# Loading the projection once and reordering the constants of a Fourier attention and mixture-of-experts kernel

## Chip, cores and metric

The kernel runs on one core of a Trainium2 chip. The core has five engines with instruction queues of their own: PE (TensorE, matrix products; PEld is its weight load), DVE (VectorE), ACT (ScalarE), POOL (GpSimd) and SP (SyncE, which here only issues DMA copies). The metric is device time in microseconds of one execution. A measurement is the median of several runs.

## What is computed

One transformer layer on x of shape (8, 512, 128): linear attention with random Fourier features over 16 heads of 8 dimensions, layer norm, then a top-2-of-8 mixture of experts (128 to 512 to 128), layer norm.

```python
q = (x @ Wq.T + bq).reshape(B, L, 16, 8)      # k and v likewise
p = einsum('blhd,dm->blhm', q, proj) / sqrt(8)
q_prime = concat([cos(p), sin(p)], -1) / sqrt(128)   # k_prime likewise
kv  = einsum('blhm,blhd->bhmd', k_prime, v)
out = einsum('blhm,bhmd->blhd', q_prime, kv)
x = layernorm(x + out.reshape(B, L, 128) @ Wo.T + bo)
route = top2(softmax(x @ Wr + br)), made to sum to 1
x = layernorm(x + sum_e route_e * (relu(x @ W1_e + b1_e) @ W2_e + b2_e))
```

The same projection, 8 x 128, serves all 16 heads.

## The kernel before

**Layout.** All work is in float32. A sequence (512 rows) is held as four chunks of 128 rows. The products that make the phases work on 32 partitions, which are four heads of 8; so the kernel keeps a block-diagonal projection `pbd`, 128 partitions by NJ * M = 4 * 128 columns: row 8h + d holds row d of proj in the column block j = h mod 4 and zeros elsewhere. `npbd` is its negative. `mask` (128 x 4) says which column block a partition belongs to; it comes from the identity `ident` by a sum on DVE (L144).

**Start.** Ahead of the planned work stands a preamble (L116 to L306):

- `load_x(0)` on SP's queue; the four weights Wq, Wk, Wv, Wo, one copy each, on ACT's queue into the tile `first` (L119).
- proj is copied 16 times, once for each head, by 16 copies on SP's queue (L150); DVE multiplies it with `mask` to `pbd` (L153) and negates it to `npbd` (L162).
- POOL fills the constants (columns such as `magic`, `halfpi`, `one`; `once`, `up`, `down`; `vm` and `kv`; `zero`, `below`, `page0` and others) and issues the copies of bv, bo, br, Wr and b2. These instructions are written on `nc.gpsimd`, whose order the framework may change.
- b1, bq and bk are copied as rows into `brow` (L184) on ACT's queue.
- `load_x(1)`, then for each expert a copy of W1 into a combined DRAM array `wcat` and one of W2 into the tile `w2` (L210), then `load_x(2)`, all on SP's queue.
- PE transposes the four weights, DVE copies them to `wT`; PE transposes `brow`, DVE copies it to `bcol` and scales two columns to `bqk`.
- POOL clears `bdiag` (L297), DVE writes b1 onto its diagonals (L298) and the negative of b1 to `nb1c` (L302), which SP stores into `wcat`.

**Planned part.** Everything after that is a list of tasks with an engine, an estimated duration, a due time counted in steps and predecessors. `Plan.make` (L1267) puts them into one order, by simulating the engines with those estimates; the wrapper `InOrder` (L70) then keeps each engine to this order. [...] The PSUM tiles of one bank each, four of them at first (L96, `banks`), are handed to tasks by the planner.

For each sequence there is a preparation (x transposed to `xT`; k, v and q by products with `wT`; `kT` written by DVE, `qT` and `xT` by ACT; `xb` = x + bo on POOL) and NS = 8 steps, four for the keys and four for the queries. A step is a phase product (`p_phase`, into the PSUM tiles `p`, called PE "p" in the profile), the turning into range and the sine and cosine (DVE and ACT), and the products with `vm` or `kv` (PE "bank"). In the first 24 steps (`TURNED`, three sequences) PE does the range reduction itself, by adding a large number, taking it off again and multiplying with `npbd`. Behind the steps come output projection, norm, routing, a scatter of rows to expert pages in DRAM, and the experts' products; pages are worked through in three groups of 4, 3 and 1 sequences.

**The shift.** Relu is done as a maximum with -b1, so what is missing is added back as one row for each expert, b1_e @ W2_e + b2_e. `prepare_shift` plans it: eight groups of four products of `bdiag` with `w2` (`p_shift`), DVE's sum with b2 (`v_shift`), the rows spread over partitions (`p_rows`, `v_rows`) and stored to `wcat`. The first group has no predecessor (`last = None`) and is due at step 9.6; in the trace one group runs ahead of k's product of sequence 0.

Of the kernel before, what the change touches and what calls it, by code (L numbers as in the profile page):

```python
# [18 lines left out]
ROUND = 12582912.0  # L19
# [6 lines left out]
def kernel(  # L26
# [57 lines left out]
    pe, act, dve, pool = (InOrder(e) for e in (nc.tensor, nc.scalar, nc.vector, nc.gpsimd))  # L84
# [14 lines left out]
    def mm(*args, **kwargs):  # L99
        pe.matmul(*args, **kwargs)  # L100

    def tr(*args):
        pe.transpose(*args)
# [12 lines left out]
    load_x(0)  # L116
    first = feat.tile([P, NG * 512], F32, tag="r", name="first")
    wnat = first[:, 0 : 4 * D].rearrange("p (i d) -> p i d", d=D)
    for i, w in enumerate((Wq, Wk, Wv, Wo)):  # L119
        nc.scalar.dma_start(out=wnat[:, i, :], in_=w)  # L120

    ident = const.tile([P, P], F32, name="ident")
    make_identity(nc, ident)

    def column(value, name):
        t = const.tile([P, 1], F32, name=name)
        nc.gpsimd.memset(t, value)
        return t
# [6 lines left out]
    mone = column(-1.0, "mone")  # L135
    one = column(1.0, "one")
    euler = column(math.e, "euler")
    low = column(-3e38, "low")

    def small_wide(t):  # L140
        return t.to_broadcast([P, NC])


    mask = const.tile([P, NJ], F32, name="mask")  # L144
    nc.vector.tensor_reduce(
        mask, ident.rearrange("p (g j d) -> p j g d", j=NJ, d=DH), AX.XY, ALU.add
    )

    prep = first[:, 4 * D : 4 * D + M]
    for h in range(H):  # L150
        nc.sync.dma_start(out=prep[DH * h : DH * (h + 1), :], in_=proj)
    pbd = const.tile([P, NJ * M], F32, name="pbd")
    nc.vector.tensor_tensor(  # L153
        pbd.rearrange("p (j m) -> p j m", m=M),
        prep.unsqueeze(1).to_broadcast([P, NJ, M]),
        mask.unsqueeze(2).to_broadcast([P, NJ, M]),
        ALU.mult,
    )


    npbd = const.tile([P, NJ * M], F32, name="npbd")
    nc.vector.tensor_scalar(npbd, pbd, -1.0, None, ALU.mult)  # L162
    once = const.tile([P, P], BF16, name="once")
    nc.gpsimd.memset(once, 1.0)
    up = const.tile([P, 1], BF16, name="up")
    nc.gpsimd.memset(up, ROUND / 32)
    down = const.tile([P, 1], BF16, name="down")
    nc.gpsimd.memset(down, -ROUND / 32)


    XW = D + DH
    vm = const.tile([P, NC, NJ * XW], F32, name="vm")
    nc.gpsimd.memset(vm, 0.0)
    kv = const.tile([P, 2, NJ * XW], F32, name="kv")
    nc.gpsimd.memset(kv, 0.0)

    def blocks(t):
        return t.rearrange("p c (j x) -> p c j x", x=XW)[:, :, :, 0:D].rearrange(
            "p c j (g y) -> p c j g y", y=32
        )[:, :, :, :, 0:DH]  # L180

    NB = E * NF
    brow = first[0 : NB + 2, 4 * D + M : 4 * D + M + P]
    nc.scalar.dma_start(out=brow[0:NB, :], in_=b1.rearrange("e (c f) -> (e c) f", f=P))  # L184
    nc.scalar.dma_start(out=brow[NB : NB + 1, :], in_=bq.unsqueeze(0))
    nc.scalar.dma_start(out=brow[NB + 1 : NB + 2, :], in_=bk.unsqueeze(0))

    bvb = const.tile([P, D], F32, name="bvb")
    nc.gpsimd.dma_start(out=bvb, in_=bv.partition_broadcast(P))
    bob = const.tile([P, D], F32, name="bob")  # L190
    nc.gpsimd.dma_start(out=bob, in_=bo.partition_broadcast(P))
    brb = const.tile([P, E], F32, name="brb")
    nc.gpsimd.dma_start(out=brb, in_=br.partition_broadcast(P))
    wr = const.tile([P, E], F32, name="wr")
    nc.gpsimd.dma_start(out=wr, in_=Wr)
    b2s = const.tile([E, D], F32, name="b2s")
    nc.gpsimd.dma_start(out=b2s, in_=b2)


    desc = const.tile([P, NC, E], F32, name="desc")  # L200
    for e in range(E):
        nc.gpsimd.memset(desc[:, :, e : e + 1], float(E - e))

    load_x(1)

# [2 lines left out]
    wcat = tc.dram_tile([E, P, WN + NF + D], F32, name="wcat")  # L208
    w2 = const.tile([P, E, NF * D], F32, name="w2")
    for e in range(E):  # L210
        nc.sync.dma_start(out=wcat[e, :, 0:FF], in_=W1[e])
        nc.sync.dma_start(
            out=w2[:, e, :].rearrange("p (c d) -> p c d", d=D),
            in_=W2[e].rearrange("(c p) d -> p c d", p=P),
        )
# [11 lines left out]
    assert L % P == 0  # L227
    DY = D + 1
    zero = const.tile([P, 8, DY], F32, name="zero")
    nc.gpsimd.memset(zero, 0.0)  # L230
    nc.gpsimd.memset(zero[:, :, D:DY].bitcast(I32), 1 << 30)
    ys_d = [tc.dram_tile([n * P, DY], F32, name=f"ys_{i}") for i, n in enumerate(pages)]
    rows = [2 * L * n for n in GROUPS]
    res_d = [tc.dram_tile([n, D], F32, name=f"res_{i}") for i, n in enumerate(rows)]
# [4 lines left out]
    row_of = const.tile([P, max(GROUPS), 2, NC], I32, name="row_of")  # L239
    for m in range(max(GROUPS)):  # L240
        for k in range(2):
            nc.gpsimd.iota(
                row_of[:, m, k, :],
                pattern=[[2, NC]],
                base=2 * L * m + k,
                channel_multiplier=2 * NC,
            )

    def clear(i, e):
# [8 lines left out]


    ones = const.tile([P, P], BF16, name="ones")  # L260
    nc.gpsimd.memset(ones, 1.0)
    ltri = const.tile([P, P], BF16, name="ltri")
    nc.gpsimd.affine_select(
        ltri, ones, pattern=[[1, P]], compare_op=ALU.is_gt, fill=0.0, base=0, channel_multiplier=-1
    )

    below = const.tile([P, E + 1, E], F32, name="below")
    nc.gpsimd.memset(below, 0.0)
    for e in range(E):
        nc.gpsimd.memset(below[:, e + 1, 0 : e + 1], 1.0)  # L270

    page0 = const.tile([P, len(GROUPS), E], F32, name="page0")
    for i in range(len(GROUPS)):
        for e in range(E):
            nc.gpsimd.memset(page0[:, i, e : e + 1], float(full[i] * e))
    ramp_i = const.tile([P, max(NT)], I32, name="ramp_i")
    nc.gpsimd.iota(ramp_i, pattern=[[1, max(NT)]], base=0, channel_multiplier=0)
    ramp = const.tile([P, max(NT)], F32, name="ramp")
    nc.gpsimd.tensor_copy(ramp, ramp_i)


    PH = [ps_p.tile([P, 2, 512], F32, tag=f"p{n}", name=f"p_{n}") for n in range(2)]
    P4 = [PH[g // 2][:, g % 2, :] for g in range(NG)]
    for i in range(4):
        tr(P4[0][:, ts(i)], wnat[:, i, :], ident)
    wT = const.tile([P, 4, D], F32, name="wT")
    dve.tensor_copy(wT.rearrange("p i d -> p (i d)"), P4[0])
    tr(P4[2][:, 0 : NB + 2], brow, ident[: NB + 2, : NB + 2])
    bcol = const.tile([P, NB + 2], F32, name="bcol")
    dve.tensor_copy(bcol, P4[2][:, 0 : NB + 2])  # L290
    scale = 1.0 / (2.0 * math.pi * math.sqrt(DH))
    bqk = const.tile([P, 2], F32, name="bqk")
    dve.tensor_scalar(bqk, bcol[:, NB : NB + 2], scale, None, ALU.mult)


    bdiag = const.tile([P, NF, E * E], F32, name="bdiag")
    nc.gpsimd.memset(bdiag, 0.0)  # L297
    nc.vector.tensor_copy(  # L298
        bdiag[:, :, :: E + 1], bcol[:, 0:NB].rearrange("p (e c) -> p c e", c=NF)
    )  # L300
    nb1c = const.tile([P, NB], F32, name="nb1c")
    nc.vector.tensor_scalar(nb1c, bcol[:, 0:NB], -1.0, None, ALU.mult)  # L302
    nc.sync.dma_start(
        out=wcat[:, :, WN : WN + NF].rearrange("e p c -> p e c"),
        in_=nb1c.rearrange("p (e c) -> p e c", c=NF),
    )  # L306
# [86 lines left out]
        )  # L393

    def prepare_shift():
        last = None
        for e in range(E):
            last = plan.add(
                "PE", 1.05, lambda bank, e=e: p_shift(bank, e), due=9.6 + e / 4,
                after=[last], bank="shift",  # L400
            )
        last = plan.add("DVE", 0.3, v_shift, due=12, after=[last], bank="shift", free="shift")
        done = []
        for e in (0, 4):
            t = plan.add("PE", 1.1, lambda bank, e=e: p_rows(bank, e), due=12.5, after=[last], bank=("rows", e))
            done.append(plan.add(
                "DVE", 0.7, lambda bank, e=e: v_rows(bank, e), due=13, after=[t],
                bank=("rows", e), free=("rows", e), ring=("r", "rows", 2),
            ))
            last = t  # L410
        t = plan.add("SP", 0.4, store_rows, due=13, after=done, land=5)
        plan.give("r", "rows", [t], lag=5)
        return t
# [788 lines left out]

    all_groups = [Group(i) for i in range(len(GROUPS))]
    seqs = [Sequence(b) for b in range(B)]
    shift_done = prepare_shift()
    clears = [(i, e) for i in range(len(GROUPS)) for e in range(E)]
    for b, s in enumerate(seqs):
        s.prepare()
        s.steps()
        for k in range(NS):  # L1210
            if clears and NS * b + k >= 1:
                i, e = clears.pop(0)
                all_groups[i].clears.append(
                    plan.add(
                        "SP", 0.3, lambda i=i, e=e: clear(i, e), due=NS * b + k,
                        after=[s.t_p[k]], land=8,
                    )
                )
# [141 lines left out]
def ts(i, size=128):  # L1360
    return slice(i * size, (i + 1) * size)
# [32 lines left out]
```

## Time and profile before

| | us |
|---|---|
| median of 3 runs | 599.53 (596.05 to 600.81) |
| the profiled execution's own time | 598.15 |
| its span, first to last instruction | 596.4 |
| PE, DVE, ACT, POOL busy | 508.1, 414.1, 352.9, 281.5 |
| first phase product starts (timeline) | 22.46 |
| a later step, phase to phase (chain: 35.84 to 40.94) | 5.1 |
| mean granted TensorE clock | 0.95 |

In the views below a line of the timeline reads: start in us from the span's start, duration, engine, line of the kernel, operation, output<-inputs, shape, count; in square brackets the idle time before it and what ended that. Several like instructions are merged into one line, with the time that they take together. L78 is the line of the `InOrder` helper, so those are told apart by their tiles. "SPq" and "ACTq" are DMA issues by the engine's queue. A line of the chain reads: start, duration, engine or DMA, output tile.

### The profile page before, as it was taken

Reading aid. Unit: us, or ns where it says so; the run is one execution under the profiler, and the core shown is the slowest. Engines: PE = TensorE matmul, PEld = TensorE weight load, DVE = VectorE, ACT = ScalarE, POOL = GpSimd, SP = SyncE. Lnnn points to the kernel's source line nnn. Section 1 sums busy time; section 2 is a strip of 40 time slices with the busy share of each in tenths; the row PEclk is TensorE's granted clock in tenths of the full one; section 3 lists DMA queues with packets and bytes.
Section 4 is the critical chain, followed back from the end, with each engine's and each line's share of the span. In section 5 each row is a group of like instructions: output and inputs, shape, how many; then the busy total and the mean of one; then the engine's idle time right before and its main releaser. Section 6 shows DMA issues by size and latency. Waiting matters only on the chain.

```text
span 596.4 us, 14279 instructions
## 1 busy us (share of the span) xinstructions
PE 508.1 (85%) x5314; PEld 335.6 (56%) x5314; DVE 414.1 (69%) x932; ACT 352.9 (59%) x278; POOL 281.5 (47%) x474
## 2 busy tenths in 40 slices
PE   1999999998898998889898997986998887978760
PEld 1465564464366456534664653564568786868760
DVE  2355577478677876967797788799668535766795
ACT  1476877876984999598989996996840000000011
POOL 9000047047056625631575476327436752576761
PEclk9999999999988999889999998998899989898995
DMA  5997069024412240132013221222334688476741
GB/s 125 327 404 275 1 226 334 10 91 135 151 45 65 79 117 9 62 83 68 10 43 111 62 72 37 81 66 68 94 96 130 174 231 290 129 239 174 262 120 70
DMA packets 48039, 77.02 MB, mean 129 GB/s; under 512 B 8191, under 2 KB 24877, under 8 KB 47972
## 3 DMA queue, kind: packets, MB, share of 16 engines
q1 hardware_dynamic: 42416, 67.26, 36.0%
q0 software_dynamic: 4928, 8.59, 4.6%
q8 instruction: 43, 0.70, 0.5%
q10 hardware_dynamic: 628, 0.28, 0.2%
q14 instruction: 24, 0.20, 0.1%
HBM read 44.62 MB, written 34.94 MB: 133 GB/s over the span
## 4 chain that ended last, share of the span: by engine, by line
PE 42%; DVE 20%; DMA 11%; ACT 9%; issue 8%; POOL 7%; SPq 3%; ACTq 0%; DVEq 0%; POOLq 0%
PE bank L78 25%; PE p L78 17%; DMA wst<-wcat 6%; DVE r L78 5%; ACT f L78 5%; ACT r L78 4%; SPq L78 2%; DVE f L78 2%; DVE hT L78 2%; POOL y L78 1%; DMA res<-og,yg 1%; POOL rs_y L78 1%; POOL ys L78 1%; DVE st L78 1%; SPq L1074 1%
## 5 line engine op out<-in xcount | busy, mean ns | idle before, releaser
L78 POOL DMA_INDIRECT res<-og,yg x85 | 92.3, 1086 | 120.4 <-DVE og L78 87.3
L78 ACT ACTIVATE f<-f,halfpi 128x2048 f32<-128x2048 f32 x64 | 128.4, 2006 | 8.1 <-DVE f L78 6.3
L78 DVE SCALAR_TENSOR_TENSOR r<-r,p 128x1024 f32<-128x1024 f32 x80 | 94.1, 1214 | 17.3 <-ACT r L78 17.2
L78 ACT ACTIVATE f<-r 128x2048 f32<-128x2048 f32 x40 | 76.5, 1913 | 25.6 <-DVE r L78 25.5
L78 ACT ACTIVATE r<-p,magic 128x1024 f32<-128x1024 f32 x80 | 84.7, 1112 | 6.4 <-PE p L78 6.3
L78 DVE TENSOR_SCALAR f<-p 128x1024 int32<-128x1024 int32 x48 | 56.7, 1220 | 42.4 <-PE p L78 36.0
L78 ACT ACTIVATE o<-acc,nb_o,rs_o 128x128 f32<-128x128 f32 x8 | 3.5, 489 | 139.2 <-DVE nb_o L78 119.6
L78 PE MATMUL bank<-f,vm 128*32 128x128 f32 x2048 | 67.6, 279 | 14.7 <-ACT f L78 14.7
L78 POOL DMA_INDIRECT ys<-y,slot_i x64 | 68.5, 1070 | 21.3 <-issue 16.1
L78 PE MATMUL bank<-yTg,wst 128*128 128x128 f32 x464 | 67.4, 292 | 7.4 <-DMA wst<-wcat 7.4
L78 PEld LDWEIGHTS bank<-f,vm 128*32 128x32 f32 x2048 | 54.2, 111 | 33.5 <-ACT f L78 18.6
L78 PE MATMUL bank<-f,kv 128*32 128x512 f32 x512 | 67.8, 619 | 5.9 <-ACT f L78 3.0
L78 PEld LDWEIGHTS bank<-yTg,wst 128*128 128x128 f32 x464 | 59.4, 201 | 22.3 <-DMA wst<-wcat 9.7
L78 PEld LDWEIGHTS bank<-w,hT 128*128 128x128 f32 x464 | 59.0, 201 | 17.6 <-DVE hT L78 7.6
L78 PE MATMUL bank<-w,hT 128*128 x464 | 66.4, 291 | 1.3 <-DVE hT L78 1.0
L78 ACT ACTIVATE f<-p 128x1024 f32<-128x1024 f32 x48 | 49.2, 1026 | 25.6 <-PE p L78 17.1
L78 POOL TENSOR_TENSOR xb<-x,bob 128x512 f32<-128x512 f32 x8 | 10.1, 1279 | 102.8 <-DVE z L78 102.8
L78 PE MATMUL p<-qT,pbd 32*128 32x512 f32 x256 | 46.6, 686 | 4.3 <-ACT f L78 2.4
L78 DVE TENSOR_SCALAR f<-r 128x2048 int32<-128x2048 int32 x40 | 49.2, 1229 | 0.2
L78 DVE TENSOR_TENSOR hT<-bank,wst 128x512 f32<-128x512 f32 x58 | 39.5, 685 | 12.0 <-PE bank L78 11.7
L78 PE MATMUL p<-pbd,kT 32*128 32x512 f32 x256 | 43.0, 639 | 3.3 <-DVE r L78 2.2
L78 PE MATMUL p<-yTg,wst 128*128 128x128 f32 x216 | 29.9, 286 | 9.4 <-DMA wst<-wcat 9.3
(192 smaller groups left out, 686.3 us busy)
## 6 DMA issues: line engine op xcount, KB each, us to landing
wst<-wcat SPq DMA_DIRECT2D x85, 322.0 KB
ys<-zero SPq DMA_DIRECT2D x29, 516.0 KB
yg<-ys SPq DMA_DIRECT2D x85, 64.5 KB
ys<-zero SPq DMA_DIRECT2D x14, 258.0 KB
got<-res SPq DMA_DIRECT2D x7, 512.0 KB
x<-in_L_attn_x_dram SPq DMA_DIRECT2D x8, 256.0 KB
wcat<-in_L_ffn_W_dram SPq DMA_DIRECT2D x8, 256.0 KB
w<-in_L_ffn_W_dram SPq DMA_DIRECT2D x8, 256.0 KB
```

The costliest lines, as they stand in the source:

```text
L78: ins = getattr(self.engine, op)(*args, **kwargs)
L1074: return nc.values_load(table[0:1, t : t + 1], engines=[engine], min_val=0, max_val=top, skip_runtime_bounds_check_because="a count of pag ...
```

## The change

- proj is copied once (8 x 128). A matrix `heads` (8 x 128, ones where a column's place within its head is the row) is made from the identity on DVE, and one product on PE, `heads` with proj, puts proj's rows under all heads, in PSUM. `pbd` is made from there by four DVE operations with the columns of `mask` as scalars; `npbd` by ACT, as -1 times `pbd`.
- The weights are copied and transposed in the order Wk, Wv, Wq, Wo. proj, bq, bk and b1 follow x0 on SP's queue. bv is copied first on POOL's queue.
- ACT takes the sine of the constant `one` among the constants. The unused column `low` goes.
- The block from `vm` to `ramp` moves behind `bqk`; the instructions written on `nc.gpsimd`, `nc.vector` and `nc.sync` in it and around it are now written on `pool`, `dve` and `sp`, the in-order wrappers. So they keep the order of the text on their engines.
- `prepare_shift` is called after the first sequence's steps have been planned, and its first group has the first phase product as its predecessor.

```diff
-    for i, w in enumerate((Wq, Wk, Wv, Wo)):
+    for i, w in ((1, Wk), (2, Wv), (0, Wq), (3, Wo)):
         nc.scalar.dma_start(out=wnat[:, i, :], in_=w)
+    proj_s = first[0:DH, 4 * D : 4 * D + M]
+    sp.dma_start(out=proj_s, in_=proj)
+    NB = E * NF
+    brow = first[0 : NB + 2, 4 * D + M : 4 * D + M + P]
+    sp.dma_start(out=brow[NB : NB + 1, :], in_=bq.unsqueeze(0))
+    sp.dma_start(out=brow[NB + 1 : NB + 2, :], in_=bk.unsqueeze(0))
+    sp.dma_start(out=brow[0:NB, :], in_=b1.rearrange("e (c f) -> (e c) f", f=P))
...
+    bvb = const.tile([P, D], F32, name="bvb")
+    pool.dma_start(out=bvb, in_=bv.partition_broadcast(P))
...
-    low = column(-3e38, "low")
+
+    table = const.tile([P, 1], F32, name="table")
+    act.activation(table, one, AF.Sin)
...
-    prep = first[:, 4 * D : 4 * D + M]
-    for h in range(H):
-        nc.sync.dma_start(out=prep[DH * h : DH * (h + 1), :], in_=proj)
     pbd = const.tile([P, NJ * M], F32, name="pbd")
-    nc.vector.tensor_tensor(
-        pbd.rearrange("p (j m) -> p j m", m=M),
-        prep.unsqueeze(1).to_broadcast([P, NJ, M]),
-        mask.unsqueeze(2).to_broadcast([P, NJ, M]),
-        ALU.mult,
-    )
...
-    nc.vector.tensor_scalar(npbd, pbd, -1.0, None, ALU.mult)
...
+    heads = const.tile([DH, P], F32, name="heads")
+    dve.tensor_copy(
+        heads.rearrange("e (h d) -> e h d", d=DH),
+        ident[0:DH, 0:DH].unsqueeze(1).to_broadcast([DH, H, DH]),
+    )
+    mm(P4[3][:, 0:M], heads, proj_s, start=True, stop=True)
+    for j in range(NJ):
+        dve.tensor_scalar(pbd[:, ts(j, M)], P4[3][:, 0:M], mask[:, j : j + 1], None, ALU.mult)
+    for i in (1, 2, 0, 3):
         tr(P4[0][:, ts(i)], wnat[:, i, :], ident)
...
+    act.activation(npbd, pbd, AF.Identity, scale=-1.0)
...
     bdiag = const.tile([P, NF, E * E], F32, name="bdiag")
-    nc.gpsimd.memset(bdiag, 0.0)
-    nc.vector.tensor_copy(
+    pool.memset(bdiag, 0.0)
+    dve.tensor_copy(
         bdiag[:, :, :: E + 1], bcol[:, 0:NB].rearrange("p (e c) -> p c e", c=NF)
     )
...
     def prepare_shift():
-        last = None
+        last = seqs[0].t_p[0]
...
-    shift_done = prepare_shift()
...
         s.steps()
+        if b == 0:
+            shift_done = prepare_shift()
```

More of the change, by code (lines that the diff above doesn't have):

```diff
@@ L144 @@
     mask = const.tile([P, NJ], F32, name="mask")
-    nc.vector.tensor_reduce(
+    dve.tensor_reduce(
         mask, ident.rearrange("p (g j d) -> p j g d", j=NJ, d=DH), AX.XY, ALU.add
     )
-    prep = first[:, 4 * D : 4 * D + M]
-    for h in range(H):
-        nc.sync.dma_start(out=prep[DH * h : DH * (h + 1), :], in_=proj)
     pbd = const.tile([P, NJ * M], F32, name="pbd")
-    nc.vector.tensor_tensor(
-        pbd.rearrange("p (j m) -> p j m", m=M),
-        prep.unsqueeze(1).to_broadcast([P, NJ, M]),
-        mask.unsqueeze(2).to_broadcast([P, NJ, M]),
-        ALU.mult,
-    )
@@ L161 @@
[L161 to L168, printed above, removed]
+    npbd = const.tile([P, NJ * M], F32, name="npbd")
+    once = const.tile([P, P], BF16, name="once")
+    pool.memset(once, 1.0)
@@ new lines @@
+    up = const.tile([P, 1], BF16, name="up")
+    pool.memset(up, ROUND / 32)
+    down = const.tile([P, 1], BF16, name="down")
+    pool.memset(down, -ROUND / 32)
+    PH = [ps_p.tile([P, 2, 512], F32, tag=f"p{n}", name=f"p_{n}") for n in range(2)]
+    P4 = [PH[g // 2][:, g % 2, :] for g in range(NG)]
+    heads = const.tile([DH, P], F32, name="heads")
+    dve.tensor_copy(
+        heads.rearrange("e (h d) -> e h d", d=DH),
+        ident[0:DH, 0:DH].unsqueeze(1).to_broadcast([DH, H, DH]),
+    )
@@ new lines @@
+    mm(P4[3][:, 0:M], heads, proj_s, start=True, stop=True)
+    for j in range(NJ):
+        dve.tensor_scalar(pbd[:, ts(j, M)], P4[3][:, 0:M], mask[:, j : j + 1], None, ALU.mult)
+    for i in (1, 2, 0, 3):
+        tr(P4[0][:, ts(i)], wnat[:, i, :], ident)
+    wT = const.tile([P, 4, D], F32, name="wT")
+    dve.tensor_copy(wT.rearrange("p i d -> p (i d)"), P4[0])
+    tr(P4[2][:, 0 : NB + 2], brow, ident[: NB + 2, : NB + 2])
+    bcol = const.tile([P, NB + 2], F32, name="bcol")
+    dve.tensor_copy(bcol, P4[2][:, 0 : NB + 2])
@@ L171 @@
+    scale = 1.0 / (2.0 * math.pi * math.sqrt(DH))
+    bqk = const.tile([P, 2], F32, name="bqk")
+    dve.tensor_scalar(bqk, bcol[:, NB : NB + 2], scale, None, ALU.mult)
+    act.activation(npbd, pbd, AF.Identity, scale=-1.0)
     XW = D + DH
     vm = const.tile([P, NC, NJ * XW], F32, name="vm")
-    nc.gpsimd.memset(vm, 0.0)
+    pool.memset(vm, 0.0)
     kv = const.tile([P, 2, NJ * XW], F32, name="kv")
-    nc.gpsimd.memset(kv, 0.0)
+    pool.memset(kv, 0.0)
     def blocks(t):
@@ L180, in blocks @@
         )[:, :, :, :, 0:DH]
[L182 to L189, printed above, removed]
     bob = const.tile([P, D], F32, name="bob")
-    nc.gpsimd.dma_start(out=bob, in_=bo.partition_broadcast(P))
+    pool.dma_start(out=bob, in_=bo.partition_broadcast(P))
     brb = const.tile([P, E], F32, name="brb")
-    nc.gpsimd.dma_start(out=brb, in_=br.partition_broadcast(P))
+    pool.dma_start(out=brb, in_=br.partition_broadcast(P))
     wr = const.tile([P, E], F32, name="wr")
-    nc.gpsimd.dma_start(out=wr, in_=Wr)
+    pool.dma_start(out=wr, in_=Wr)
     b2s = const.tile([E, D], F32, name="b2s")
-    nc.gpsimd.dma_start(out=b2s, in_=b2)
+    pool.dma_start(out=b2s, in_=b2)
     desc = const.tile([P, NC, E], F32, name="desc")
     for e in range(E):
-        nc.gpsimd.memset(desc[:, :, e : e + 1], float(E - e))
+        pool.memset(desc[:, :, e : e + 1], float(E - e))
     load_x(1)
@@ L210 @@
     for e in range(E):
-        nc.sync.dma_start(out=wcat[e, :, 0:FF], in_=W1[e])
-        nc.sync.dma_start(
+        sp.dma_start(out=wcat[e, :, 0:FF], in_=W1[e])
+        sp.dma_start(
             out=w2[:, e, :].rearrange("p (c d) -> p c d", d=D),
@@ L229 @@
     zero = const.tile([P, 8, DY], F32, name="zero")
-    nc.gpsimd.memset(zero, 0.0)
-    nc.gpsimd.memset(zero[:, :, D:DY].bitcast(I32), 1 << 30)
+    pool.memset(zero, 0.0)
+    pool.memset(zero[:, :, D:DY].bitcast(I32), 1 << 30)
     ys_d = [tc.dram_tile([n * P, DY], F32, name=f"ys_{i}") for i, n in enumerate(pages)]
@@ L241 @@
         for k in range(2):
-            nc.gpsimd.iota(
+            pool.iota(
                 row_of[:, m, k, :],
@@ L260 @@
     ones = const.tile([P, P], BF16, name="ones")
-    nc.gpsimd.memset(ones, 1.0)
+    pool.memset(ones, 1.0)
     ltri = const.tile([P, P], BF16, name="ltri")
-    nc.gpsimd.affine_select(
+    pool.affine_select(
         ltri, ones, pattern=[[1, P]], compare_op=ALU.is_gt, fill=0.0, base=0, channel_multiplier=-1
@@ L267 @@
     below = const.tile([P, E + 1, E], F32, name="below")
-    nc.gpsimd.memset(below, 0.0)
+    pool.memset(below, 0.0)
     for e in range(E):
-        nc.gpsimd.memset(below[:, e + 1, 0 : e + 1], 1.0)
+        pool.memset(below[:, e + 1, 0 : e + 1], 1.0)
     page0 = const.tile([P, len(GROUPS), E], F32, name="page0")
@@ L274 @@
         for e in range(E):
-            nc.gpsimd.memset(page0[:, i, e : e + 1], float(full[i] * e))
+            pool.memset(page0[:, i, e : e + 1], float(full[i] * e))
     ramp_i = const.tile([P, max(NT)], I32, name="ramp_i")
-    nc.gpsimd.iota(ramp_i, pattern=[[1, max(NT)]], base=0, channel_multiplier=0)
+    pool.iota(ramp_i, pattern=[[1, max(NT)]], base=0, channel_multiplier=0)
     ramp = const.tile([P, max(NT)], F32, name="ramp")
[L279 to L293, printed above, removed]
+    pool.tensor_copy(ramp, ramp_i)
     bdiag = const.tile([P, NF, E * E], F32, name="bdiag")
-    nc.gpsimd.memset(bdiag, 0.0)
-    nc.vector.tensor_copy(
+    pool.memset(bdiag, 0.0)
+    dve.tensor_copy(
         bdiag[:, :, :: E + 1], bcol[:, 0:NB].rearrange("p (e c) -> p c e", c=NF)
@@ L301 @@
     nb1c = const.tile([P, NB], F32, name="nb1c")
-    nc.vector.tensor_scalar(nb1c, bcol[:, 0:NB], -1.0, None, ALU.mult)
-    nc.sync.dma_start(
+    dve.tensor_scalar(nb1c, bcol[:, 0:NB], -1.0, None, ALU.mult)
+    sp.dma_start(
         out=wcat[:, :, WN : WN + NF].rearrange("e p c -> p e c"),
```

## Prediction

> **What bounds the kernel now.** I read the page first, then the chain of work that ended last over the first 30 us, then the timeline there. The page says that no engine is full over the whole span and that the chain changes hands all the time:
>
> ```profile
> span 596.4 us, 14279 instructions
> ...
> PE 508.1 (85%) x5314; PEld 335.6 (56%) x5314; DVE 414.1 (69%) x932; ACT 352.9 (59%) x278; POOL 281.5 (47%) x474
> ...
> PE 42%; DVE 20%; DMA 11%; ACT 9%; issue 8%; POOL 7%; SPq 3%; ACTq 0%; DVEq 0%; POOLq 0%
> ```
>
> So nothing in the steady part has room that this change touches; its edits all lie ahead of the first phase product or move small products behind it. The chain of the start, in order of time, is what matters:
>
> ```profile
> 5.74 3.73 DMA first<-in_L_attn_proj_mat_dram
> 9.47 0.02 issue
> 9.49 2.27 DMA x<-in_L_attn_x_dram
> 11.76 2.88 DVE pbd L153
> ...
> 14.65 0.43 DVE npbd L162
> 15.08 0.60 DVE wT L78
> ...
> 16.22 6.30 PE bank L78 x20
> 22.53 2.36 PE p L78 x24
> ```
>
> Here pbd stands still until 11.76, and everything on DVE and then PE waits behind it: the first phase product of sequence 0 ("PE p") starts at 22.5. From there on it is step after step, about 5.1 us each (30.74, 35.84, 40.94 are the starts of the products behind three phases in that chain), so an earlier first phase should reach the end almost whole. The timeline of the same stretch shows why pbd is late, and a second thing:
>
> ```profile
> 1.26 7.13 SPq L151 DMA_DIRECT2D first<-in_L_attn_proj_mat_dram  x16
> ...
> 9.49 0.36 SPq L78 DMA_DIRECT2D x<-in_L_attn_x_dram  x1
> ...
> 10.52 0.37 POOL L297 MEMSET bdiag<- 128x256 f32 x1
> ...
> 11.51 2.52 POOL L78 TENSOR_TENSOR xb<-x,bob 128x512 f32<-128x512 f32 x2
> ...
> 11.74 2.88 DVE L153 TENSOR_TENSOR pbd<-first,mask 128x512 f32<-128x512 f32 x1 [9.63 <-DMA x<-in_L_attn_x_dram]
> ...
> 13.93 0.74 POOL L78 COPY y<-row_of 128x8 int32<-128x8 int32 x1
> ...
> 18.03 2.08 PE L78 MATMUL bank<-xT,wT 128*128 128x512 f32 x2
> ```
>
> and, a little later in the same view,
>
> ```profile
> 22.46 1.14 PE L78 MATMUL p<-pbd,kT 32*128 32x512 f32 x8
> ```
>
> SP spends 7.13 us on issuing 16 small copies, 0.45 each. And pbd takes 2.88 us, although DVE's other 128x512 operations on two operands take 0.69 (z<-bank,xb): it starts inside POOL's two xb additions (11.51 to 14.02) and ends 0.6 after them. DVE was held off by POOL.
>
> **The change, part by part, up to the first phase.**
>
> *Issues.* SP now issues x0 (0.80), one copy of proj (1.26), bq, bk and b1, at 0.45 each: done near 3.1, so x1 goes at 3.1 instead of 9.49, and the 16 W1/W2 copies (9.89 to 20.5 now) follow 6.4 us earlier. ACT's queue loses three issues. proj lands by about 4.4 (1.26 plus the 3.16 of Wq in the chain), b1 between 4.4 and 5.8 (2.65 plus 1.72, its time now, or 3.16).
>
> *PE and DVE.* heads needs ident (ready at 1.8) behind mask (to 2.1), so about 2.3. The product heads x proj is 0.45 (median of the transposes out of first): 4.4 to 4.85. Four weight transposes 1.1 to 1.5, row transpose 0.29, x transposes 1.11: about 7.4. pbd becomes four DVE operations of 128x128 out of PSUM, 0.285 each (row vm<-bank,bvb): 4.85 to 6.0; wT 0.68, bcol 0.18, bqk 0.17: 7.0, hidden behind PE's x transposes. npbd moves to ACT, 0.69 like qT, from 6.0: done at 6.7, before xT's input is there (7.4), so it costs nothing; if pbd came a microsecond later it would push xT by as much. The sine's table load (1.28) goes from 23.27, where it lies under the first phase (22.46 to 24.9), to about 3: nothing either way. xT 0.60: k can start at 8.1. From k's start to the first phase the present trace needs 22.46 - 18.03 = 4.43 us (k, v, q), so PE alone would be ready at 12.5.
>
> *A rule on PE's clock.* k's two matmuls take 2.08 us here, and 1.02 to 1.13 later on. The Trainium skill's "TensorE: Matmul & The Clock Gate" (Part 1) has PE at half rate until it has been busy for about 3.4 us, and back there after an idle window as long. With shift's first product gone from in front of k, that speaks against the change: k, v and q may all run cold, 2.08 + 2.2 + 2.08 = 6.4 instead of 4.43, and PE is ready at 14.5. By the row alone it is 12.5. I take 13; it decides only if nothing else is later, and the next paragraph is.
>
> *POOL, now in program order, and the wait that it hands on.* bvb's issue (0.78) only moves forward. But bdiag's memset, which the present trace has at 10.52 in the middle of POOL's list, becomes its last item before xb. The same work ends at 11.51 now; four dependent pairs (zero, ltri, below, ramp) now stand back to back, about 0.1 each (dependent 0.20 us operations in the normalisation start 0.28 apart), so bdiag ends near 12.1 and the two xb additions begin near 12.0. DVE, also in order, has bdiag's copy and nb1c ahead of kT, and kT stands ahead of the first phase.
>
> Is that small copy held off by xb, as pbd was? By the row nearest to it, no: pbd has two SBUF inputs, the copy one. Then kT runs from 12.4 to 13.15 and the first phase starts at 13.2. By the Trainium skill's "SBUF — State Buffer" ("Who interferes with whom"), yes: one-source copies and tensor_scalar within SBUF also take the pair of ports that POOL uses, whoever comes first keeps it for its whole instruction and the other fully blocks. One trace row supports that rule: POOL's acc<-y takes 0.87 us beside DVE's y<-y copy (82.9) and 0.61 where DVE is doing something else (397.4). So I take the rule: bdiag and nb1c wait until 12.0 + 2.52 = 14.5, take 0.25, kT 0.75: 15.5, first phase at 15.55. PE is idle for some 2.5 us before it, shorter than the window above, so no second cold start is charged (bound: +1.2, half of a phase product). This needs bob, whose copy POOL issues at about 5.4, to have landed by 12.0. It took 4.6 us in quiet; a 64 KB scatter takes a median 5.1 us to land with the queues full (94 to 106 us) against 2.3 later (181 to 195), so 10 to 12.8 with W1/W2 streaming beside it. More often in time than not.
>
> Gain at the first phase: 22.46 - 15.55 = 6.9 us.
>
> *After the first phase.* The eight groups of shift products are the same work, 1.04 each. One of them (16.22, 1.87 us long) lay on the present starting chain and is already inside the 22.46; now it lies behind the first phase, in the gaps of the steps. A gap with products and one shift group is 2.74 us long in the chain (33.48 minus 30.74), where ACT and DVE alone would need about 2.5; so a group costs 0.25 where it fits and 1.04 where it does not. I take 0.5. shift's bank is held anyway; the rows follow one gap later (stored at 82.0 now), and the first weights are fetched at 142.5, so 60 us cover that. The earlier W1/W2 copies keep ahead of their users by the same distance (w2[0] lands near 9, its product comes near 18.5). heads costs one product and one copy in idle time.
>
> **Sum.** 6.9 - 0.5 = 6.4 us. The profiled execution took 598.15 us (span 596.4, 1.75 around it): 591.75. It lies 1.4 below the median of the three runs shown, 599.53; against that the time is 593.1.
>
> **Rivals.**
>
> (1) *No block by xb* (bob late, or the small copies slip through). For it: the only blocked DVE row has two inputs. First phase at 13.2, gain 9.3 - 0.5 = 8.8: 590.7. If proj lands earlier and PE is warm by the x transposes, no more than 1.5 us more, 589; if PE stays cold instead (14.5), 592.
>
> (2) *The start is earlier, the end is not.* The gain is given back later, in a lower granted clock (1.00 until 100 us, 0.87 at 160 to 200, mean 0.95) or in a replanned order: PE is 42% of the chain, 250 us, and a mean clock lower by 0.02 costs 5.3 us. Against it: the work per step is unchanged. 597 to 599. That the edits fail to shorten the start at all is the same case: the heads product and DVE's wait behind bdiag would have to eat all of it.
>
> (3) *Slower: shift's place in the plan.* The products are tied behind the first phase and share the four banks with x, k, v and q of sequences 1 and 2. If the shift bank, free at 60.6 now (shift<-bank,b2s), is released a full step late just when sequence 2's x, sequence 0's attention output and z want banks (64.75 to 74), each step that misses its bank costs 5.1 us. One missed step gives back most of the gain; from two on (10.2 us) it is a loss, and three give 599.5 - 6.4 + 15.3 = 608. Against it: 7 of 8 groups already sit in such gaps and the chain there goes on evenly.
>
> **How the numbers follow.** Likeliest case, 45%: 593.1, by itself from 590.5 to 595.5 (runs of the kernel before scatter from 596.05 to 600.81). Rival 1 and its further ends 33%, 589 to 592. Rival 2 13%, 597 to 600. Rival 3 9%, 606 to 610. The range 588.5 to 598 leaves out rival 3, half of rival 2 and a little below. A measurement of this kernel can tell about 1%, 6 us, from no change: the line is at 593.5, just above the likeliest. Somewhat more than half of the likeliest case (25 of 45) and 30 of rival 1's 33 count as faster, 55%; slower by over 1% is rival 3, 9%; the rest, 36%, within.
>
> **What would show it.** In the profile after: x1 issued near 3; pbd's four pieces over by 6.5; k near 8; bdiag's copy on DVE beginning or ending near 14.6, next to two xb additions (right) or done by 12.5 (rival 1); the first p product near 15.5; steps of 5.1 us behind it; shift<-bank,b2s about one gap later relative to the first phase. Wrong would be a first phase after 18, or a step in sequences 0 to 2 that lasts 10 us, or a first phase at 15 with an end that has not moved.

## The result and the profile after

The changed kernel takes 592.37 us (median of 20 runs, 586.74 to 597.98); the kernel before, beside it on the same chip, 596.71 us (20 runs, 594.25 to 600.81). The ratio is 0.9909, 95% interval 0.9881 to 0.9937: 5.4 us less, between 3.8 and 7.1, a gain of under 1%. The ratio is that of the mean times without slow runs (here one of the changed kernel, 597.98 us, at a granted clock of 0.94), so it differs from that of the medians, which are 4.3 us apart. The profiled execution took 591.92 us.

First the page of the changed kernel: its span, the busy times, and the shares by engine of the chain that ended last.

```profile
span 590.2 us, 14273 instructions
...
PE 505.8 (86%) x5316; PEld 334.6 (57%) x5316; DVE 416.1 (70%) x935; ACT 351.9 (60%) x279; POOL 280.9 (48%) x473
...
PE 43%; DVE 21%; DMA 9%; ACT 9%; issue 8%; POOL 7%; SPq 3%; ACTq 0%; DVEq 0%; POOLq 0%
```

The engines' busy times are those of before to within 2.3 us. The span is 6.2 shorter, and of the chain's shares only DMA has lost, from 11% to 9%. At the start the chain held 10.9 us of copies before (3.16 + 1.72 + 3.73 + 2.27) and holds 4.8 now (2.88 + 1.93): a wait went, not work. Next the chain of the changed kernel over the start (start, duration, engine or DMA, output tile).

```profile
3.69 1.93 DMA first<-in_L_ffn_b_dram
...
5.64 0.81 PE p L78 x2
...
6.47 1.14 DVE pbd L78 x4
...
9.06 0.60 ACT xT L78
...
9.71 4.77 PE bank L78 x12
14.47 2.36 PE p L78 x24
```

The projection's copy is gone from the chain, pbd begins at 6.47 instead of 11.76, and PE's phase products follow directly on q at 14.47 where they stood at 22.53. The chain gives the start of PE's first product (5.64) to a copy of b1, `first<-in_L_ffn_b_dram`. The timeline of the same stretch says the same of the product, but gives its weight load (PEld) to `heads`:

```profile
1.77 0.78 POOL L78 DMA_DIRECT2D bvb<-in_L_attn_bv_dram  x1
...
1.98 3.60 DVE L78 COPY heads<-ident 8x128 f32<-8x128 f32 x1
...
2.61 1.94 POOL L78 MEMSET vm<- 128x2176 f32 x1
...
4.05 0.42 SPq L78 DMA_DIRECT2D x<-in_L_attn_x_dram  x1
...
4.46 1.04 POOL L78 MEMSET kv<- 128x1088 f32 x1
...
5.64 0.50 PEld L78 LDWEIGHTS p<-first,heads 8*128 8x128 f32 x2 [5.64 <-DVE heads L78]
5.64 0.79 PE L78 MATMUL p<-first,heads 8*128 8x128 f32 x2 [5.64 <-DMA first<-in_L_ffn_b_dram]
...
6.47 1.13 DVE L78 TENSOR_SCALAR pbd<-p,mask 128x128 f32<-128x128 f32 x4 [0.89 <-PE p L78]
...
7.63 0.63 ACT L78 ACTIVATE npbd<-pbd 128x512 f32<-128x512 f32 x1 [3.46 <-DVE pbd L78]
...
9.71 2.08 PE L78 MATMUL bank<-xT,wT 128*128 128x512 f32 x2 [0.69 <-ACT xT L78]
...
12.08 2.52 POOL L78 TENSOR_TENSOR xb<-x,bob 128x512 f32<-128x512 f32 x2
...
12.14 1.25 DVE L78 COPY bdiag<-bcol 128x32 f32<-128x32 f32 x1 [3.29 <-POOL bdiag L78]
...
13.28 1.19 PE L78 MATMUL bank<-xT,wT 128*128 128x512 f32 x2
13.30 0.17 DVE L78 TENSOR_SCALAR nb1c<-bcol 128x32 f32<-128x32 f32 x1
13.39 0.74 DVE L78 TENSOR_SCALAR kT<-bank,bcol 128x512 f32<-128x512 f32 x1
...
14.40 1.14 PE L78 MATMUL p<-pbd,kT 32*128 32x512 f32 x8
```

Four things are to be seen. `heads`, a copy of 8 partitions by 128, takes 3.60 us and ends at 5.58, just after POOL's `kv` at 5.50: it, and not b1 (landed at 5.62, within 0.04 us of it), should be what PE's product waited for; e1 below shows that it was. k runs at 9.71 (before: 18.03) in the slow 2.08 us. bdiag's copy takes 1.25 us and ends when the first of the two xb additions does (13.39 and 13.34); `nb1c` then slips in between the two, and `kT` follows it. And the first phase product begins at 14.40, right after q's (13.28 plus 1.19; PE's records overlap a little), while kT had been over for 0.3: PE's own queue came last, not kT.

**How far the lead carries.** The lead is the start of a step's first product in the kernel before minus that in the changed one: 8.06 us for steps 0 to 7, 7.15 for steps 10 to 22, between 6.4 and 8.9 from then to the last step (63: 429.05 before, 420.16 after), 6.2 at the span's end. The 0.91 is given back where the displaced group of shift products lies. Engine by engine the order of instructions differs only up to about step 12, and is the same behind it.

### The profile page after: what moved, and what is told of

Same layout as the page of the kernel before. It is cut to its first block, busy times and chain, and to the rows that moved or that the text cites. A ratio compares the mean times of both kernels' runs of the same rounds, so it can differ in the third digit from the quotient of the medians.

```text
span 590.2 us, 14273 instructions
## 1 busy us (share of the span) xinstructions
PE 505.8 (86%) x5316; PEld 334.6 (57%) x5316; DVE 416.1 (70%) x935; ACT 351.9 (60%) x279; POOL 280.9 (48%) x473
## 4 chain that ended last, share of the span: by engine, by line
PE 43%; DVE 21%; DMA 9%; ACT 9%; issue 8%; POOL 7%; SPq 3%; ACTq 0%; DVEq 0%; POOLq 0%
PE bank L78 24%; PE p L78 19%; ACT f L78 5%; DVE r L78 4%; DMA wst<-wcat 4%; ACT r L78 4%; DVE hT L78 2%; POOL ys L78 2%; DVE f L78 2%; SPq L78 2%; DMA ys<-y,slot_i 2%; POOL y L78 1%; DVE acc L78 1%; DMA yg<-ys 1%; DVE st L78 1%
## 5 line engine op out<-in xcount | busy, mean ns | idle before, releaser
L78 DVE SCALAR_TENSOR_TENSOR r<-r,p 128x1024 f32<-128x1024 f32 x80 | 94.0, 1212 | 15.7 <-ACT r L78 15.7
L78 PE MATMUL bank<-yTg,wst 128*128 128x128 f32 x464 | 65.9, 288 | 4.4 <-DMA wst<-wcat 4.4
L78 PEld LDWEIGHTS bank<-yTg,wst 128*128 128x128 f32 x464 | 58.2, 197 | 18.3 <-issue 7.6
L78 PE MATMUL p<-yTg,wst 128*128 128x128 f32 x216 | 30.5, 289 | 12.2 <-DMA wst<-wcat 12.0
```

The costliest lines, as they stand in the source:

```text
L78: ins = getattr(self.engine, op)(*args, **kwargs)
```

## Experiments

The kernel before was run beside each set; a ratio is always to it, on the same chip. Every kernel here computes all that the changed kernel computes.

**e1: heads without the one-source copy.**

```diff
-    dve.tensor_copy(
+    dve.tensor_tensor(
         heads.rearrange("e (h d) -> e h d", d=DH),
         ident[0:DH, 0:DH].unsqueeze(1).to_broadcast([DH, H, DH]),
+        ident[0:DH, 0:DH].unsqueeze(1).to_broadcast([DH, H, DH]),
+        ALU.mult,
     )
```

> The changed kernel, with heads made by DVE as ident times ident (two SBUF inputs, no two-port copy). If POOL's memsets held the copy's write port (3.60 us in the changed kernel), heads is done near 2.2 instead of 5.58, since memsets do not read; the first product then waits only for proj's landing. If that is near 4.4, PE's chain comes 1.2 us earlier (k near 8.5), but kT still waits for bdiag's copy behind xb (13.4), so the first phase starts near 14.2 instead of 14.40 and the time stays within 0.5 us of the changed kernel's. Rival: PE was waiting for b1's copy (5.62) and nothing moves. Second rival: the long copy is not POOL's doing, and the product of two takes as long.

Measured: 593.05 us (10 runs), ratio 0.9920 (0.9882 to 0.9958). The timeline of e1's start:

```profile
1.98 0.27 DVE L78 TENSOR_TENSOR heads<-ident 8x128 f32<-8x128 f32 x1
...
4.00 0.76 PE L78 MATMUL p<-first,heads 8*128 8x128 f32 x2 [4.00 <-DMA first<-in_L_attn_proj_mat_dram]
4.01 0.32 SPq L78 DMA_DIRECT2D first<-in_L_ffn_b_dram  x1
...
8.14 2.07 PE L78 MATMUL bank<-xT,wT 128*128 128x512 f32 x2 [0.69 <-ACT xT L78]
...
12.14 1.25 DVE L78 COPY bdiag<-bcol 128x32 f32<-128x32 f32 x1 [4.94 <-POOL bdiag L78]
...
13.31 1.29 DVE L78 TENSOR_SCALAR nb1c<-bcol 128x32 f32<-128x32 f32 x1
...
14.52 0.74 DVE L78 TENSOR_SCALAR kT<-bank,bcol 128x512 f32<-128x512 f32 x1
...
15.31 1.14 PE L78 MATMUL p<-pbd,kT 32*128 32x512 f32 x8 [1.68 <-DVE kT L78]
```

The same output takes 0.27 instead of 3.60. Now proj is the last to come (4.00), before b1's copy has even been issued (4.01), so b1 is not what this product needs; and k stands at 8.14, where the prediction had it. Yet the first phase is *later* than in the changed kernel, 15.31, because here nb1c too lost to the second xb addition (1.29 against 0.17) and kT came at 14.52. So in this kernel the step that I predicted for the changed one happened nearly to the letter (kT to 15.26, first phase 15.31; predicted 15.5 and 15.55). Freeing heads alone gains next to nothing, as long as bdiag's copy stands ahead of kT.

**e4: the two small operations freed as well.** e1, and bdiag's copy and nb1c read the transposed biases where PE left them, in PSUM, instead of their copy `bcol` in SBUF:

```diff
-        bdiag[:, :, :: E + 1], bcol[:, 0:NB].rearrange("p (e c) -> p c e", c=NF)
+        bdiag[:, :, :: E + 1], P4[2][:, 0:NB].rearrange("p (e c) -> p c e", c=NF)
...
-    dve.tensor_scalar(nb1c, bcol[:, 0:NB], -1.0, None, ALU.mult)
+    dve.tensor_scalar(nb1c, P4[2][:, 0:NB], -1.0, None, ALU.mult)
```

> e1 and also bdiag and nb1c read out of PSUM instead of from bcol in SBUF, so that neither is a one-source operation within SBUF. If the port rule holds, bdiag's write starts when POOL's memset ends (12.1) and is over in 0.2 us, not 1.25; kT follows k directly, and with k near 8.5 the first phase starts at 13.2, 1.2 us before the changed kernel's: 591. Rival: proj or b1 lands late, PE's own chain stays, first phase 14.4, time as the changed kernel's.

Measured: 589.46 us (6 runs), ratio 0.9873 (0.9824 to 0.9921). The timeline of e4:

```profile
12.08 2.49 POOL L78 TENSOR_TENSOR xb<-x,bob 128x512 f32<-128x512 f32 x2
12.14 0.22 DVE L78 COPY bdiag<-p 128x32 f32<-128x32 f32 x1 [4.78 <-POOL bdiag L78]
12.25 0.18 DVE L78 TENSOR_SCALAR nb1c<-p 128x32 f32<-128x32 f32 x1
12.35 0.74 DVE L78 TENSOR_SCALAR kT<-bank,bcol 128x512 f32<-128x512 f32 x1
...
13.55 1.14 PE L78 MATMUL p<-pbd,kT 32*128 32x512 f32 x8
```

Same start, same xb beside it, only the source is another memory: 0.22 instead of 1.25 and 0.18 instead of 1.29 in e1. So bdiag and nb1c waited because their source was in SBUF while POOL was adding. For heads, e1 changed the form of the operation and not POOL's work. That the copy ended 0.08 us after kv's memset in each of its four profiles (here, e3, e5, e10) points the same way, but no run has this copy without POOL beside it, so there the cause is in part argued. The Trainium skill's "SBUF — State Buffer" ("Who interferes with whom") agrees with what was measured: copies and tensor_scalar within SBUF can, where their operands allow the faster modes that need it, take the pair of ports shared with POOL; an operation with at most one SBUF input outside those modes does not meet POOL (bdiag from PSUM, 0.22); and one with two SBUF inputs meets only a POOL instruction that reads (e1's heads, 0.27 beside POOL's descriptors and memsets).

**e2 and e3: the two halves of the change, each alone.** e2 is the kernel before with only `prepare_shift` in its new place, the last two pieces of the change's diff.

> The kernel before with only prepare_shift's new place. The planned order becomes that of the changed kernel. k no longer stands behind a shift group and bdiag: it starts near 15.7 (wT ready) instead of 18.03, the first phase near 20.1 instead of 22.46; 0.9 us is given back where the displaced group lands (steps 8 to 10). So 1.4 us below the kernel before, 595 to 595.5. Rival (the new plan costs several microseconds in the later part, which is why only 4 to 5 of the 8 us arrive at the end): 597 to 600, slower than before although the first phase is earlier.

Measured: 594.71 us (13 runs), ratio 0.9945 (0.9920 to 0.9970); k at 15.84, first phase at 20.84, lead 1.62, and 0.73 behind the displaced group. A gain of 3.3 us from a lead of 0.73 fits nothing, so the same kernel was run again as e6:

> e2 once more: its lead is 1.6 us at the first phase and 0.7 behind the displaced shift group, yet 3.3 us were measured. If that was scatter, now 0.996 to 1.000 of before; if the place of the shift group does something for the later part that the start's lead doesn't show, again 0.993 to 0.996.

Measured: 595.91 us (12 runs), ratio 0.9980 (0.9946 to 1.0014), first phase 20.30, lead 2.16, then 1.27. The extra gain of e2 did not come back. The two intervals overlap: it was scatter between sets of runs.

e3 is the changed kernel with those two pieces turned round, so that one group of shift products stands ahead of k again:

> The changed kernel with prepare_shift where it was, so its planned order is the one of before. One shift group stands ahead of k on PE again and waits for bdiag's copy, which waits for xb: bdiag near 13.4, the group to 15.3, k from there, the first phase near 13.4 + 6.2 = 19.7 instead of 14.40. It does not pay the 0.9 us later. So about 4.4 us above the changed kernel: 596.5 to 597, some 2.7 us of the first phase's gain left against before, with as little as 0.5 to be seen. Rival (the loading alone makes the gain, the shift's place only costs): as fast as the changed kernel or faster, 591 to 592.

Measured: 596.95 us (14 runs), ratio 0.9963 (0.9932 to 0.9994), first phase 19.28, lead 3.18 kept to the end of the early steps. The timeline of e3:

```profile
12.14 1.25 DVE L78 COPY bdiag<-bcol 128x32 f32<-128x32 f32 x1 [3.29 <-POOL bdiag L78]
...
13.44 1.88 PE L78 MATMUL bank<-w,bdiag 128*8 128x128 f32 x8 [4.43 <-DVE bdiag L78]
...
15.24 2.08 PE L78 MATMUL bank<-xT,wT 128*128 128x512 f32 x2
...
19.28 1.14 PE L78 MATMUL p<-pbd,kT 32*128 32x512 f32 x8
```

With the shift products in the old place PE stands still for 4.43 us until bdiag is written, and bdiag hangs on POOL's last memset and then, for 1.25 us, on xb. k, behind them in PE's order, begins at 15.24 instead of 9.71, and of the changed kernel's 8.06 us at the first phase 3.18 are left.

**e5: the changed kernel again**, unaltered.

> The changed kernel once more, on the same chip as the next three. First phase at 14.4 or at 15.3: which of the two, nb1c or POOL's second xb addition, gets the pair of ports at 13.3 is decided by a hair, and e1 and e3 lost there what the changed kernel's profile won. If the lead at the first phase is carried to the end one for one, the ratio to before is 0.988 (7.1 us), and the 5.4 us measured are its scatter; if the later part takes something back each time, again 0.990 to 0.991.

Measured: 592.8 us (6 runs), ratio 0.9885 (0.9825 to 0.9945). The timeline of e5:

```profile
12.14 0.20 DVE L78 COPY bdiag<-bcol 128x32 f32<-128x32 f32 x1 [3.29 <-POOL bdiag L78]
12.23 2.54 POOL L78 TENSOR_TENSOR xb<-x,bob 128x512 f32<-128x512 f32 x2
...
12.33 0.74 DVE L78 TENSOR_SCALAR kT<-bank,bcol 128x512 f32<-128x512 f32 x1
...
13.27 1.89 PE L78 MATMUL bank<-xT,wT 128*128 128x512 f32 x2
...
15.08 1.14 PE L78 MATMUL p<-pbd,kT 32*128 32x512 f32 x8
```

The same code, the third outcome: here bdiag's copy came first (0.20 us) and xb had to wait for it, so kT ran at 12.33. The first phase is at 15.08 all the same, because q ran slow (1.89 against 1.19 in the first profile). Its lead behind the shift group is 6.47.

**e7 and e8: how early can it be?** e8 is e4 with the memset of bdiag moved to POOL's list ahead of vm:

```diff
     pool.memset(down, ...)
+    bdiag = const.tile([P, NF, E * E], F32, name="bdiag")
+    pool.memset(bdiag, 0.0)
```

e7 is e8 with five products of the identity with itself on PE (four before heads, one before k), to have PE at full rate when k comes. They are added work whose output nothing reads.

> e4, with bdiag cleared by POOL ahead of vm, so that DVE can write it and nb1c right behind bqk and kT waits for k alone; and with PE kept busy by four products of ident with itself ahead of the heads product and one in front of k, into a PSUM bank that nobody reads then. [...]k (near 8.3) now takes 1.04 instead of 2.07, v 1.16, q 1.02, and the first phase starts near 11.6 instead of 13.55: 2 us below e4. Rival: transposes and such fillers do not count as busy, k stays at 2.07 and the first phase at 13.5; or the fillers end late and push k back by up to 1 us.

> e7 without the fillers. kT is ready by 11.2, yet the first phase still stands behind v and q on a cold PE: 13.5, as e4. Time as e4 within 0.5 us, about 0.987 of before. If the first phase comes earlier, kT and not PE's own queue was the bound in e4.

Measured: e8 589.01 us (6 runs), ratio 0.9848 (0.9796 to 0.9901); e7 591.38 us (6 runs), ratio 0.9873 (0.9813 to 0.9933). First the timeline of e7, then that of e8:

```profile
1.80 2.07 PE L78 MATMUL p<-ident 128*128 128x128 f32 x8 [1.80 <-POOL ident masks.py:199]
...
8.30 2.07 PE L78 MATMUL bank<-xT,wT 128*128 128x512 f32 x2 [0.26 <-ACT xT L78]
...
11.48 1.02 PE L78 MATMUL bank<-xT,wT 128*128 128x512 f32 x2
```

```profile
7.02 0.21 DVE L78 COPY bdiag<-p 128x32 f32<-128x32 f32 x1
...
8.06 2.07 PE L78 MATMUL bank<-xT,wT 128*128 128x512 f32 x2 [0.69 <-ACT xT L78]
...
10.18 0.75 DVE L78 TENSOR_SCALAR kT<-bank,bcol 128x512 f32<-128x512 f32 x1 [2.87 <-PE bank L78]
...
11.57 1.02 PE L78 MATMUL bank<-xT,wT 128*128 128x512 f32 x2
...
12.53 1.14 PE L78 MATMUL p<-pbd,kT 32*128 32x512 f32 x8
```

In e8 kT now follows k directly, and the first phase is set by PE alone: 12.53, a lead of 9.93, 9.03 behind the shift group. The fillers of e7 did next to nothing (first phase 12.43): k takes its slow 2.07 although PE had work almost without a gap from 1.80 to 8.04. By "TensorE: Matmul & The Clock Gate" (Part 1), about 3.4 us of sustained work should have been enough. Its Part 4 adds that transposes do not count as work in the same way, and from 4.76 to 7.40 PE did transposes; the products before them fill 3.0 us (1.80 to 4.83). That would fit, but no run here separates it.

e8 against the changed kernel, once more and side by side. In this set every kernel took 5 to 6% longer than in the others, with the same course up to 94 us (steps 8 to 14 of e10 start 1.0 later than in the first profile of that code, its step 16 then 7.5 later). The profile puts the wait that begins there down to "remote" and names no cause, and only the ratios are compared:

> The kernel of e8 once more, timed beside the changed kernel on one chip. If the time at the end follows the first phase one for one: first phase 12.5 to 13.5 in the profile (PE's step to full rate comes at another moment in each execution), ahead of the kernel before by 8 to 9 us behind the displaced shift group, and the median 8 to 9 us below the kernel before (ratio 0.985 to 0.987). If the start is partly given back later: no more than 6 us below, as the changed kernel was.

> The changed kernel once more, as the partner of e9. If the time follows the first phase one for one: first phase 14.4 to 15.6, 6 to 7 us below the kernel before (ratio 0.988 to 0.990), and so about 2 us above e9. If part is given back: about 5 us below the kernel before, and no difference to e9 outside the intervals.

Measured: e9 (e8's kernel) 622.71 us, ratio 0.9868 (0.9838 to 0.9897), first phase 12.78; e10 (the changed kernel) 621.98 us, ratio 0.9888 (0.9842 to 0.9935), first phase 15.12; the kernel before 630.47 us. The 2 us between them that the first phases let expect did not show in the medians. e8's kernel beats the kernel before in both sets. By the ratios it beats the changed one by 2.2 us in one set and 1.3 in the other, both well within the intervals: its advantage of some 2 us is in the trace, but not shown in the time.

## Why the prediction was right, step by step

In the main the mechanism was right: the projection's late copy held up the start, and an earlier start reaches the end almost whole. The gain was 5.4 us (3.8 to 7.1) where 6.4 was forecast. That the time itself lies only 0.7 us below the forecast of 593.1 is in part luck: the forecast stands on 599.53, the median of three runs, and over 20 runs the kernel before takes 596.71. The first phase came 1.15 us earlier than forecast (14.40 for 15.55), and there two terms of the start were wrong and cancelled in part.

**The last wait before the first phase: not the one forecast.** The forecast has the later of two: PE, ready at 13, and kT, held behind bdiag until 15.5. In all three profiles of this code kT was over first (14.13, 13.07, 14.13 in the first profile, e5 and e10), and the first phase followed directly on q's products (14.40, 15.08, 15.12). PE was late because heads was; kT was early because xb held it for less. The sizes: with heads on time and the wait as it was, the first phase would stand at about 14.2 (an estimate, from kT's end at 14.13), so the wait was taken 1.4 too long; heads, with q's slow products behind it, then moves it to 14.9, the mean of the three, 0.7 that the forecast lacked. e1 is the run in which the forecast's own wait did come last.

**heads at 2.3, its product at 4.4: wrong.** I had the copy ready as soon as `ident` was, and left out that it is a one-source copy within SBUF, while POOL issues bvb's copy and clears vm and kv. It is the very rule that I applied to bdiag's copy ten microseconds later; I did not go through DVE's other small operations with it. The copy ended at 5.58, k at 9.71 instead of 8.1. e1 shows the rest of that sum to be right: proj lands by 4.00 (4.4 predicted), k at 8.14.

**bdiag and nb1c wait for both xb additions, until 14.5: right in kind, half in size.** In this profile they waited for the first only. Over the profiles in which this stretch is the same kT started at 12.33 (e5), 13.39 (the first profile, and e10) and 14.52 (e1): it is decided by which of the two engines comes first at 12.1 and 13.3. The rule held each time; which of the three outcomes comes, I could not have known, and a range over all three would have been the honest form of that step.

**PE from k to the first phase: 4.9 us taken (8.1 to 13), about right.** Where the first phase followed q directly the profiles have 4.0 us (e3) to 5.4 (e5 and e10, in the same code in which the first profile had 4.7), for the bounds 4.43 and 6.4. k ran slow in every profile; what differed was whether q, and part of v, still did. The granted clock in the views reads 1.00 throughout the start and does not show this. But the first clock record in each trace is one of full clock, and where it begins fits: at 13.6 us in the first profile, 15.0 in e5 and 15.7 in e10, with k at 9.7 in all three and q taking 1.19, 1.89 and 1.91. So the clock rule did speak against the change, by up to 1 us (5.4 for 4.43).

**Costs taken as nothing: right.** npbd on ACT (0.63 us) ended 0.8 before xT began. The sine's table load now runs from 2.68 to 3.97, before ACT has anything to do. bob landed at 11.8 (6.4 us after its issue at 5.41), 0.3 before xb began; in e7 xb had to wait for it. x1 was issued at 4.05 rather than 3.1, as b1's issue in front of it waited until 3.69, just when Wk's copy landed (3.68); nothing waited for x1. The kernel before had such waits too, so its 7.13 us on SP were not all issuing, as I read them: an issue of proj takes 0.27 to 0.38 us, and between the third and the fourth SP waited 1.5. In both kernels SP and ACT had issued eight copies when the wait began; what sets that is not shown.

**The shift group: 0.91 instead of 0.5**, between the bounds 0.25 and 1.04, nearer to the upper one. shift<-bank,b2s came one gap later, as predicted (57.65 against 60.61 before, which is 5.1 later once the 8.06 of the first phase is taken off).

**Rival 1 (no block)** is what e4 and e8 make. In e5 the changed kernel did it by itself, kT at 12.33, but with the end that the rival had named for a PE that stays cold: first phase 15.08, 592.8 us (592 predicted). **Rival 3 (shift misses banks, steps of 10 us)** did not happen: no step between 0 and 22 is late by more than the 0.91. **Rival 2 (given back later)**: the table sets the lead behind the shift group against the time.

| kernel | first phase | lead behind shift group | time gained (ratio times the median before) |
|---|---|---|---|
| e2, e6: only shift's place | 20.84, 20.30 | 0.73, 1.27 | 3.3, 1.2 |
| e3: only the start | 19.28 | 3.18 | 2.2 (0.4 to 4.1) |
| changed, e5 | 14.40, 15.08 | 7.15, 6.47 | 5.4 (3.8 to 7.1), 6.9 (3.3 to 10.5) |
| e1 | 15.31 | 6.25 | 4.8 (2.5 to 7.1) |
| e4 | 13.55 | 8.0 | 7.6 (4.7 to 10.5) |
| e7 | 12.43 | 8.7 | 7.6 (4.0 to 11.2) |
| e8 | 12.53 | 9.03 | 9.1 (5.9 to 12.2) |

But for e2, every lead lies in the interval of its time or at its edge, and lead minus gain averages 0.3 us over the nine measurements of the table (0.7 without e2). A systematic loss behind the start is not needed. (All leads are to the one profile of the kernel before. e9 and e10, whose set runs at another pace from 94 us on, are left out; up to there they lead by 8.8 and 6.2, for gains of 8.3 and 7.1.) What single profiles show there is scatter: from step 24 to the end the kernel before needs 441.8 us, the changed one 442.4, e1 440.0, e2 439.2, e3 443.2, e4 440.6, in no order of the change. One place where the two profiles differ is in the windows of the last phase of work, first of the changed kernel, then of the one before (length, busy time of PE, PEld, DVE, ACT, POOL, granted clock, DMA share, GB/s):

```profile
450.00:500.00 50.00, 41.08 (x310) 38.74 (x309) 24.76 (x63) 0.00 (x0) 26.67 (x29) 0.91 0.73 216
```

```profile
450.00:500.00 50.00, 43.45 (x351) 41.38 (x351) 28.40 (x80) 0.40 (x1) 31.94 (x41) 0.97 0.66 189
```

In this one pair the granted clock is 0.91 against 0.97 (the stretches hold not quite the same work). Over the 19 runs of the changed kernel that the ratio uses, the time falls with the mean granted clock (correlation -0.58; 0.01 of clock goes with about 2.3 us), and the runs scatter with a standard deviation of 2.5 us. Whether the change itself takes something of the clock stays open; the means of the two profiled executions, 0.951 and 0.950, give no sign of it.

**The two halves need each other.** With the old start and the old plan the first phase is at 22.46; shift's new place alone brings it to 20.3 to 20.8 (1.6 to 2.2 us), the new start alone to 19.28 (3.2), both to 14.4 to 15.1 (7.3 to 8.1). The sum of the single gains is 4.8 to 5.3. The rest exists only together: with the projection late, k still begins only at 15.84 (e2); with the shift products in front of k, PE waits for bdiag (e3's 4.43 us) however early the projection is.

## What to carry to other kernels

When a late copy at the start is taken away, go through the order of every engine behind it: the gain ends at the next item that waits for something else. Here that was, from run to run, PE's own slow products or kT behind bdiag's memset at the end of POOL's list; moving that memset forward and freeing the small operations brought the first phase to 12.53 (e8). Check each small DVE copy or tensor_scalar within SBUF for POOL work beside it, the new ones too; a source in PSUM, or a form with two inputs beside memsets, took the wait away here, 1.25 us to 0.22 and 3.60 to 0.27. And test the parts of a change together as well as singly: here each part alone gave less than half of the lead at the first phase.

## What the runs showed of the hardware that was not expected

- A copy of 8x128 elements took 3.60 us beside POOL's descriptors for bvb and its memsets of vm and kv, in all four profiles with that copy. POOL's instructions there follow each other without a gap (bvb to 2.55, the next from 2.54; vm from 2.61 to 4.55, kv from 4.46), and DVE did not come through between them.
- Between two additions on POOL, DVE's small operation sometimes came through (nb1c 0.17 us) and sometimes not (1.29 us), in code that was the same there.
- PE work from 1.80 to 8.04 us, matrix products and transposes, did not bring PE to full rate: k took 2.07 us at 8.30. The first record of full clock begins at 11.0 in e7 and 11.5 in e8, but at 14.4 in e1 and 15.0 in e5, although k began at 8.14 and 9.69 there. Counted from k's start that is 2.6 us (e3, where the shift products run in front of k) to 6.3 (e1) over the twelve profiles, and 3.9, 5.3 and 6.0 in the three of one and the same code (the changed kernel, e5, e10), whose first phase so varied by 0.7 us with nothing changed.
